# One-by-one row loads on two engines instead of one, with shared DMA semaphores and fewer gather buffers

## The chip, the cores and the metric

The kernel runs on one core of one Trainium2 chip. Times are device microseconds of that core. Five engines work beside each other, each through its own in-order queue: TensorE (PE; its weight loads are listed as PEld), VectorE (DVE), ScalarE (ACT), GpSimd (POOL) and the sync engine (SP). SP computes nothing; it issues DMAs. ScalarE can issue DMAs too, and GpSimd issues the indirect ones, whose source rows are given by a list of indices.

## The reference

One layer of a graph network: 12500 nodes with 128 features, 200000 edges sorted by their target node.

```python
h = jnp.maximum(_layernorm(x, axis=-1), 0.0)
msgs = h[src]
agg = jax.ops.segment_sum(msgs, dst, num_segments=n)
deg = jax.ops.segment_sum(jnp.ones((src.shape[0],)), dst, num_segments=n)
agg = agg / jnp.maximum(deg, 1.0)[:, None]
y = jax.nn.relu(agg @ Wg + h @ Ws + bg)
y = jnp.tanh(y @ W1 + b1)          # 128 -> 512
y = jnp.tanh(y @ W2 + b2)          # 512 -> 512
out = x + (y @ W3 + b3)            # 512 -> 128
```

All is float32. The irregular part is `h[src]`: 200000 rows of 512 bytes in the order of the edges.

## The kernel before

**Setup** (to about 111 us). The normalised rows h are computed in pieces and written to a table in DRAM, `htab`. The edge list is turned into columns, so that a column of `scol` holds the 128 source nodes of one chunk.

**Chunks.** The edges are cut into 1563 chunks of 128. Since the targets are sorted, a chunk's targets fall in a window of 144 nodes. For each chunk TensorE multiplies the 128 gathered rows by a 128 x 144 matrix of zeros and ones, which VectorE makes for groups of eight chunks (`onehot`, lines 360 to 383), and adds the product into a PSUM accumulator (`add`, line 422). 512 nodes are a block; 64 chunks feed one block. When its sums are complete, the block goes through the three layers (`part0` to `part4`, lines 516 to 583): matmuls on TensorE, with relu, tanh and bias on ScalarE between them.

**Where a chunk's rows come from.** There are three kinds.
- 1465 chunks are gathered: one indirect DMA of 128 rows each, issued by POOL (`gather`, line 301) into one of `AHEAD` = 48 buffers. A gather is issued up to 48 gathered chunks ahead of the add, and needs the buffer of an earlier chunk to be free.
- 80 raw chunks take rows of x itself, gathered at the start and normalised later.
- 18 "slow" chunks, one after every 72 gathered ones from chunk 160 on, are loaded row by row (`row_loads`, line 327). SP reads 32 row addresses into registers at a time (line 333), then, for each row, sets a register and issues a DMA of 512 bytes (line 341). Four buffers are kept for such chunks.

**The order of the work.** One loop over the chunks (line 632) writes the whole order out. In each turn it may issue a store, make the zeros and ones of a later group, issue gathers, let SP do its next four rows (line 655: one batch of four per 2.25 gathered chunks), add the chunk, and on every second chunk do one step of a block's layers. `keep_in_program_order` holds the instructions of TensorE, ScalarE and SP in this order, each on its own engine. SP's queue thus holds, mixed with the rows, the loads of `hb` and `xb` (h and x of a block) and the stores of `o` (results). From chunk `QUICK` = 1376 on, the layers' steps are placed by a small planner, which takes a chunk's rows to be there at 7.5 us plus 1.251 us for each gather before it (line 658), and a slow chunk's rows to be there already.

DMAs of SP and ScalarE count their completion on eight semaphores, taken in turn. A DMA waits until the last DMA on its semaphore, eight places earlier, has landed.

Of the kernel before, what the change touches and what calls it, by code (L numbers as in the profile page):

```python
# [22 lines left out]
F32 = mybir.dt.float32  # L23
# [8 lines left out]
P = 128  # L32
# [5 lines left out]
NRAW = 10  # L38
RAW0 = 256
STEP = 40  # L40
AHEAD = 48
SLOW0 = 160
EACH = 72
TOGETHER = 4
LOADS = 32
LATE = 12
LEAD = 16
QUICK = 1376
# [11 lines left out]
def windowed(ctx, tc, x, src, dst, Wg, Ws, bg, W1, b1, W2, b2, W3, b3, out, flag):  # L60
    nc = tc.nc
    N, D = x.shape
# [18 lines left out]
    def raw(c):  # L81
        return RAW0 <= c < RAW1 and (c - RAW0) % STEP < GRP


    slow, n = [], 0
    for c in range(SLOW0, NCH - 12):
        if raw(c):
            continue
        if n <= 0:
            slow.append(c)  # L90
            n = EACH
        else:
            n -= 1


    def first(w, span=per):
# [8 lines left out]
    blocks, n = [], 0  # L105
# [10 lines left out]
    rows_one = ctx.enter_context(tc.tile_pool(name="rows_one", bufs=4))  # L116
    rows_in = ctx.enter_context(tc.tile_pool(name="rows_in", bufs=AHEAD))
    ps_c = ctx.enter_context(tc.tile_pool(name="ps_c", bufs=1, space=PSUM))
# [8 lines left out]
    for t, a in ((rsrc, src), (rdst, dst)):  # L127
        a = a[RAW0 * P : RAW1 * P].rearrange("(u e) -> u e", u=NRAW)[:, : GRP * P]
# [46 lines left out]
    def centre(pool, xt, k, stats, bufs=2):  # L175
        nc.vector.tensor_reduce(stats[:, 0], xt, AX.X, ALU.add)
        nc.vector.scalar_tensor_tensor(xt, spread(stats[:, 0], k), -1.0 / D, xt, op0=ALU.mult, op1=ALU.add)
        sq = pool.tile([P, k, D], F32, name=f"sq{k}", bufs=bufs)
        nc.scalar.activation(sq, xt, AF.Square)
        nc.vector.tensor_reduce(stats[:, 1], sq, AX.X, ALU.add)  # L180

    def factors(stats):
        nc.scalar.activation(stats[:, 1], stats[:, 1], AF.Sqrt, bias=eps, scale=1.0 / D)
        nc.vector.reciprocal(stats[:, 1], stats[:, 1])
# [4 lines left out]
    with tc.tile_pool(name="setup", bufs=1) as sp, tc.tile_pool(name="ln", bufs=2) as ln:  # L189
# [59 lines left out]
        for c0, w in WINDOWS[1:]:  # L249
            v = low[:, c0:]  # L250
# [44 lines left out]
    def flat(t):  # L295
        return t.rearrange("p a b -> p (a b)")

    def sp_dma(*a):
        tc.keep_in_program_order(nc.sync.dma_start(*a))

    def gather(c):
        r = rows_in.tile([P, D], F32, name="rows")
# [7 lines left out]
    ROWB = 4 * D  # L310
    hbytes = htab.rearrange("n d -> (n d)").bitcast(U8)
# [3 lines left out]
    place = const.tile([len(slow), P], I32, name="place")  # L315
# [8 lines left out]
        def copy(*a):  # L324
            tc.keep_in_program_order(nc.scalar.copy(*a))

    def row_loads():
        for i, c in enumerate(slow):
            r = rows_one.tile([P, D], F32, name="srows")
            rows_t[c] = r  # L330
            rb = r.bitcast(U8)
            for p0 in range(0, P, LOADS):
                loads, vs = nc.values_load_multi_w_load_instructions(
                    place[i : i + 1, p0 : p0 + LOADS], engines=[mybir.EngineType.SP], min_val=0,
                    max_val=(N - 1) * ROWB,
                    skip_runtime_bounds_check_because="src holds rows of x, as the indirect DMAs take it to",
                )
                for ld in loads:
                    tc.keep_in_program_order(ld)
                for p, v in enumerate(vs, p0):  # L340
                    sp_dma(rb[p : p + 1, :], hbytes[bass.ds(v, ROWB)].rearrange("(o b) -> o b", o=1))
                    if (p + 1) % TOGETHER == 0:
                        yield

    def raw_stats(i):
        return stats_raw[:, :, i * GRP : (i + 1) * GRP]

    def raw_scaled(i):
        h = raw_rows[i]
        scale(h, h, GRP, raw_stats(i))  # L350
        for j in range(GRP):
            rows_t[RAW0 + i * STEP + j] = h[:, j]
# [11 lines left out]
    def onehot(g):  # L364
        k = min(GRP, NCH - g * GRP)
        lo, w = window(g * GRP)
        is_raw = raw(g * GRP)
        oh = ed.tile([P, GRP, W_RAW], F32, name="ohr", bufs=2) if is_raw else oh_bufs[g % OHS]
        if not is_raw and w < oh_w[g % OHS]:
            nc.vector.memset(oh[:, :, w : oh_w[g % OHS]], 0.0)  # L370
            oh_w[g % OHS] = w
        nc.vector.tensor_tensor(  # L372
            oh[:, :k, :w], lane[:, None, :w].to_broadcast([P, k, w]),
            dloc[:, g * GRP : g * GRP + k][:, :, None].to_broadcast([P, k, w]), op=ALU.is_equal,
        )
        ohs[g] = oh
        step, n = (oh.shape[2], w) if is_raw else (PITCH - per, w + per * (k - 1))
        cnt = ed.tile([P, PITCH], BF16, name="cnt", bufs=16)
        part, row, col = oh.ap
        shifted = bass.AP(tensor=oh.tensor, offset=oh.offset, ap=[part, [col[0], n], [step * col[0], k]])  # L380
        with nc.allow_low_precision(reason="whole numbers up to the chunks of a group"):
            nc.vector.tensor_reduce(cnt[:, :n], shifted, AX.X, ALU.add)  # L382
        counts[g] = (lo, n, cnt)
# [10 lines left out]
    def count(b):  # L394

        n, m = blocks[b]
        dg = flat(ps_m.tile([P, 4, P], F32, name="pm"))
        groups = sorted({c // GRP for c in reach[b]})
        for g in groups:
            lo, w, cnt = counts[g]  # L400
            a0, a1 = max(lo, n), min(lo + w, n + m)
            pe.matmul(
                dg[:, a0 - n : a1 - n], ones, cnt[:, a0 - lo : a1 - lo], start=(g == groups[0]), stop=(g == groups[-1]),
                skip_group_check=True,
            )
        rd = ml.tile([P, BLK], F32, name="rd", bufs=3)
        nc.vector.tensor_scalar(rd[:, :m], dg[:, :m], 1.0, None, op0=ALU.max)  # L407
        nc.vector.tensor_reduce(total[:, b : b + 1], dg[:1, :m], AX.X, ALU.add)
        nc.vector.reciprocal(rd[:, :m], rd[:, :m])  # L409
        rds[b] = rd  # L410
# [189 lines left out]
        )  # L600

    order = [c for c in range(NCH) if not raw(c) and c not in slow]
    loading = row_loads()
    work, done, nxt, behind = [], 0, 0, 0
    ngrp = -(-NCH // GRP)
    span = BLK // per
# [2 lines left out]
    def store(upto):  # L609
        while stores and stores[0][0] <= upto:  # L610
            sp_dma(*stores.pop(0)[1:])

    def soonest():
        two = work[: 2 if len(work) > 1 and work[1][3] < work[0][3] and work[0][4] else 1]
        return min(two, key=lambda w: max(w[2], now), default=None)
# [16 lines left out]
    for c in range(NCH):  # L632
        g = c // GRP
        at = c
        store(c if c >= QUICK else c - LATE)
        if c % GRP == 0 and g + 2 < ngrp:
            onehot(g + 2)
            if raw((g + 2) * GRP):
                raw_scaled(((g + 2) * GRP - RAW0) // STEP)
            if 2 <= g < 2 + NRAW:  # L640
                centre(ed, raw_rows[g - 2], GRP, raw_stats(g - 2), bufs=1)
            if g == 2 + NRAW:
                factors(stats_raw)

        while c % GRP == GRP // 2 and counted < len(blocks) and reach[counted][-1] // GRP <= g + (c >= QUICK):
            count(counted)
            counted += 1
        while nxt < len(order) and nxt < behind + AHEAD:
            gather(order[nxt])
            nxt += 1  # L650
        if not raw(c) and c not in slow:
            behind += 1
            batch = behind * P // (EACH * TOGETHER)
            if behind > SLOW0 - 3 * EACH and batch > (behind - 1) * P // (EACH * TOGETHER):
                next(loading, 0)
        if c >= QUICK:

            there = 7.5 + 1.251 * (NRAW * GRP + order.index(c)) if c not in slow else 0
            while soonest() and max(now, soonest()[2]) < there:
                go_on(soonest())  # L660
            now = max(now, there) + 0.27
        add(c)

        lead = LEAD if c < QUICK else 2
        if done < len(blocks) and (c - lead if across[done] else c) >= reach[done][-1]:
            if across[done]:
                merge(done)
            quick = reach[done][-1] + LEAD >= QUICK

            before = done - 1 if done and reach[done - 1][-1] + LEAD < QUICK else None  # L670
            work.append([layers(done, before), 0, 0, 0, quick and blocks[done][1] <= P])
            done += 1

        if c % span == span - 10 and (c // span + 1) * BLK < N:
            own_turned(c // span + 1)
            if (c // span + 2) * BLK < N:
                own(c // span + 2)
        if c < QUICK:
            if c % 2 == 0:
                go_on(work[0] if work else None)  # L680
        if c == QUICK:
            for b, (_, n) in enumerate(blocks):
                if n < BLK:
                    own_part(b)
# [379 lines left out]
```

## Time and profile before

| | |
|---|---|
| median of 15 runs | 2343.8 us (2334.72 to 2350.2) |
| the profiled execution | 2338.67 us, span 2336.7 us |
| mean TensorE clock granted | 0.784 of full speed |
| POOL: gathers from `htab` | 1465, first at 111.0, last at 2277.7 us |
| SP: row DMAs | 2304, first at 118.8, last at 2083.8 us |
| ScalarE: work | 226.8 us in 362 instructions |
| DMA engines, busy | 20% of the time between 111 and 2279 us |

How to read the lines of the profile: "busy" is an engine's own work; what a sequencer does (waits, register moves, issuing DMAs) is not counted there and stands under the queue's name with a q, as SPq. In a line of waits, the first name waited for the second: total us, times, longest. In a line of the order of time come start, duration, engine, source line, operation, result and operands, number of instructions, and in brackets the idle time before it and what ended that. In the view of one tile or source line the three durations are the shortest, the median and the longest in ns, then the first and last start in us. All matmuls and DMAs recorded by a helper carry that helper's line: L290 for matmuls, L299 for SP's DMAs, L322 for activations, L303 for gathers.

### The profile page before, as it was taken

Reading aid. Unit: us, or ns where it says so; the run is one execution under the profiler, and the core shown is the slowest. Engines: PE = TensorE matmul, PEld = TensorE weight load, DVE = VectorE, ACT = ScalarE, POOL = GpSimd, SP = SyncE. Lnnn points to the kernel's source line nnn. Section 1 sums busy time; section 2 is a strip of 40 time slices with the busy share of each in tenths; the row PEclk is TensorE's granted clock in tenths of the full one; section 3 lists DMA queues with packets and bytes.
Section 4 is the critical chain, followed back from the end, with each engine's and each line's share of the span. In section 5 each row is a group of like instructions: output and inputs, shape, how many; then the busy total and the mean of one; then the engine's idle time right before and its main releaser. Section 6 shows DMA issues by size and latency. Waiting matters only on the chain.

```text
span 2336.7 us, 19720 instructions
## 1 busy us (share of the span) xinstructions
PE 1330.9 (57%) x5212; PEld 872.7 (37%) x5212; DVE 1066.2 (46%) x651; ACT 226.8 (10%) x362; POOL 1463.9 (63%) x1553
## 2 busy tenths in 40 slices
PE   0132345567657766765565654555665566564768
PEld 0021233344335444443343333333333343332437
DVE  5924283455446545643353443434444444423432
ACT  1100010001111011100001000000000000010013
POOL 7675656666666666666666666666666666646660
PEclk9998577778878787787777777877777777776789
DMA  6721111212221222212222122222121221221210
GB/s 167 214 53 38 50 46 50 55 51 60 56 57 53 54 55 59 60 52 55 54 55 54 52 55 55 55 56 52 53 62 50 57 57 51 54 59 44 63 49 10
DMA packets 124131, 139.34 MB, mean 60 GB/s; under 512 B 32776, under 2 KB 98454, under 8 KB 123816
## 3 DMA queue, kind: packets, MB, share of 16 engines
q0 software_dynamic: 49440, 101.35, 16.6%
q1 hardware_dynamic: 71374, 33.32, 5.2%
q10 hardware_dynamic: 3196, 3.32, 0.6%
q8 instruction: 43, 0.70, 0.1%
q14 instruction: 78, 0.64, 0.1%
HBM read 125.06 MB, written 12.82 MB: 59 GB/s over the span
## 4 chain that ended last, share of the span: by engine, by line
PE 36%; another core or an unknown queue 25%; DVE 16%; issue 16%; POOL 5%; ACT 1%; DMA 0%; DVEq 0%; POOLq 0%; ACTq 0%
PE pm L290 22%; PE agg L290 9%; DVE cnt L382 7%; PE edge L290 5%; DVE oh L372 5%; POOL raw L146 3%; POOL rows L303 2%; DVE rd L409 2%; PE pt L293 1%; ACT h L322 1%; DVE o L579 0%; DMA rows<-htab,scol 0%; DVE mT L523 0%; DVE rd L407 0%
## 5 line engine op out<-in xcount | busy, mean ns | idle before, releaser
L303 POOL DMA_INDIRECT rows<-htab,scol x1465 | 1385.4, 946 | 788.5 <-issue 336.2
L290 PE MATMUL pm<-h,w 128*128 128x512 f32 (+4 forms) x1344 | 716.5, 628 | 172.5 <-ACT h L322 97.5
L372 DVE TENSOR_TENSOR oh<-shared,dloc 128x1152 f32<-128x1152 f32 (+2 forms) x186 | 243.5, 1315 | 875.0 <-remote 373.0
L290 PE MATMUL agg<-oh,rows 128*128 128x144 f32 (+3 forms) x2098 | 442.2, 330 | 261.3 <-issue 206.1
L290 PEld LDWEIGHTS agg<-oh,rows 128*128 128x128 f32 x2098 | 389.5, 226 | 511.3 <-issue 445.0
L382 DVE TENSOR_REDUCE cnt<-oh 128x200 bf16<-128x1600 f32 (+2 forms) x186 | 524.7, 2825 | 4.8
L290 PEld LDWEIGHTS pm<-h,w 128*128 128x128 f32 x1344 | 241.4, 218 | 214.6 <-issue 106.6
L290 PEld LDWEIGHTS edge<-oh,rows 128*128 128x128 f32 x832 | 152.4, 219 | 135.9 <-issue 131.3
L290 PE MATMUL edge<-oh,rows 128*128 128x144 f32 (+2 forms) x832 | 163.3, 317 | 28.9 <-issue 26.7
L293 PE MATMUL pt<-ident,hb 128*128 128x128 f32 x98 | 26.7, 411 | 265.5 <-DVE o L579 178.5
L322 ACT ACTIVATE h<-pm,b2c 128x512 f32<-128x512 f32 (+4 forms) x112 | 70.8, 633 | 694.5 <-PE agg L290 222.3
L293 PEld LDWEIGHTS pt<-ident,hb 128*128 128x128 f32 x98 | 16.7, 206 | 273.7 <-DVE o L579 182.9
L290 PE MATMUL pm<-mT,wg 128*128 128x512 f32 (+4 forms) x56 | 45.2, 904 | 104.0 <-DVE mT L523 82.5
L407 DVE TENSOR_SCALAR rd<-pm 128x512 f32<-128x512 f32 (+4 forms) x28 | 17.4, 621 | 175.6 <-remote 123.2
L322 ACT ACTIVATE h<-pm,b1c 128x512 f32<-128x512 f32 (+4 forms) x112 | 68.7, 632 | 259.8 <-remote 185.6
L146 POOL DMA_INDIRECT raw<-in_x_dram,rsrc x80 | 77.6, 970 | 25.6 <-issue 24.1
L409 DVE RECIPROCAL rd<-rd 128x512 f32<-128x512 f32 (+4 forms) x28 | 81.8, 2920 | 0.0
L290 PE MATMUL pm<-cnt,ones 128*128 128x200 bf16 (+7 forms) x294 | 30.5, 227 | 47.1 <-issue 46.9
L290 PEld LDWEIGHTS pm<-mT,wg 128*128 128x128 f32 x56 | 12.1, 268 | 110.2 <-DVE mT L523 86.3
L205 PE MATMUL pm<-ident,idx_f 98*128 98x98 f32 x32 | 6.2, 376 | 75.8 <-issue 75.8
L322 ACT ACTIVATE h<-pm,bgc 128x512 f32<-128x512 f32 (+4 forms) x28 | 17.7, 632 | 294.8 <-remote 120.3
L579 DVE TENSOR_TENSOR o<-pt,xb 128x512 f32<-128x512 f32 x23 | 15.8, 686 | 60.6 <-remote 45.0
(68 smaller groups left out, 509.9 us busy)
## 6 DMA issues: line engine op xcount, KB each, us to landing
srows<-htab SPq DMA_DIRECT2D x2304, 0.5 KB
rows<-htab,scol POOLq DMA_INDIRECT x1465
hb<-htab SPq DMA_DIRECT2D x24, 256.0 KB
xb<-in_x_dram SPq DMA_DIRECT2D x23, 256.0 KB
out_dram<-o SPq DMA_DIRECT2D x23, 256.0 KB
htab<-h SPq DMA_DIRECT2D x6, 896.0 KB
xt<-in_x_dram SPq DMA_DIRECT2D x5, 896.0 KB
raw<-in_x_dram,rsrc POOLq DMA_INDIRECT x80
```

Of the source, the lines that this page charges most:

```text
L146: nc.gpsimd.indirect_dma_start(out=t[:, j, :], out_offset=None, in_=x, in_offset=bass.IndirectOffsetOnAxis(ap=rsrc[:, g, j : j + 1], axis=0),)
L205: nc.tensor.transpose(p[:, q, :NROW], rf[:, (q0 + q) * P : (q0 + q + 1) * P], ident[:NROW, :NROW])
L290: tc.keep_in_program_order(nc.tensor.matmul(*a, **k))
L293: tc.keep_in_program_order(nc.tensor.transpose(*a, **k))
L303: nc.gpsimd.indirect_dma_start(out=r, out_offset=None, in_=htab, in_offset=bass.IndirectOffsetOnAxis(ap=scol[:, c : c + 1], axis=0),)
L322: tc.keep_in_program_order(nc.scalar.activation(*a, **k))
L372: nc.vector.tensor_tensor(oh[:, :k, :w], lane[:, None, :w].to_broadcast([P, k, w]), dloc[:, g * GRP : g * GRP + k][:, :, None].to_broadcas ...
L382: nc.vector.tensor_reduce(cnt[:, :n], shifted, AX.X, ALU.add)
L407: nc.vector.tensor_scalar(rd[:, :m], dg[:, :m], 1.0, None, op0=ALU.max)
L409: nc.vector.reciprocal(rd[:, :m], rd[:, :m])
L579: nc.vector.tensor_tensor(o[:, :whole], po[:, :whole], xb[:, :whole], op=ALU.add)
```

## The change

Row-by-row loading is done by two engines. From chunk 160 on, a chunk goes to SP after every 48 others (instead of 72), and to ScalarE after every 60 others, the first after 24, up to chunk 1436. That makes 27 chunks for SP (3456 rows) and 19 for ScalarE (2432 rows), and leaves 1437 for POOL. ScalarE's batches of four rows stand in its queue between the activations. Each engine has four buffers for such chunks; gather buffers go from 48 to 44. A new helper, `in_turn`, keeps all of these DMAs, of both engines, in one order for the assignment of semaphores: it adds an ordering mark without a wait between each such DMA and the one before it in the program. The index rows that ScalarE loads during setup (`at_i`, line 314) go from 18 to 46.

```diff
-AHEAD = 48
+AHEAD = 44
 SLOW0 = 160
-EACH = 72
+EACH = 48
+EACH_A = 60
...
-    slow, n = [], 0
+    slow_s, slow_a = [], []
+    ns, na = 0, EACH // 2
     for c in range(SLOW0, NCH - 12):
         if raw(c):
             continue
-        if n <= 0:
-            slow.append(c)
-            n = EACH
+        if ns <= 0:
+            slow_s.append(c)
+            ns = EACH
+        elif na <= 0 and c < QUICK + EACH_A:
+            slow_a.append(c)
+            na = EACH_A
         else:
-            n -= 1
+            ns -= 1
+            na -= 1
+    slow = slow_s + slow_a
...
+    turn = []
+
+    def in_turn(start):
+
+        tc.keep_in_program_order(start)
+        if turn:
+            tc.add_manual_dep(
+                start.ins, turn.pop(),
+                mybir.DependencyInfo(mybir.DependencyClass.NoSync, mybir.DependencyReason.DATA), reason="in_turn",
+            )
+        turn.append(start.ins.name)
+
     def sp_dma(*a):
-        tc.keep_in_program_order(nc.sync.dma_start(*a))
+        in_turn(nc.sync.dma_start(*a))
...
+        def dma(*a):
+            in_turn(nc.scalar.dma_start(*a))
+
-    def row_loads():
-        for i, c in enumerate(slow):
-            r = rows_one.tile([P, D], F32, name="srows")
+    def row_loads(chunks, engine, dma, name, together):
+        for c in chunks:
+            i = slow.index(c)
+            r = rows_one.tile([P, D], F32, name=name)
...
-                    if (p + 1) % TOGETHER == 0:
+                    dma(rb[p : p + 1, :], hbytes[bass.ds(v, ROWB)].rearrange("(o b) -> o b", o=1))
+                    if (p + 1) % together == 0:
                         yield
...
-    loading = row_loads()
+    loading = row_loads(slow_s, mybir.EngineType.SP, sp_dma, "srows", TOGETHER)
+    loading_a = row_loads(slow_a, mybir.EngineType.Activation, act.dma, "arows", TOGETHER)
...
             if behind > SLOW0 - 3 * EACH and batch > (behind - 1) * P // (EACH * TOGETHER):
                 next(loading, 0)
+            batch = behind * P // (EACH_A * TOGETHER)
+            if behind > 48 and batch > (behind - 1) * P // (EACH_A * TOGETHER):
+                next(loading_a, 0)
```

More of the change, by code (lines that the diff above doesn't have):

```diff
@@ L333, in row_loads @@
                 loads, vs = nc.values_load_multi_w_load_instructions(
-                    place[i : i + 1, p0 : p0 + LOADS], engines=[mybir.EngineType.SP], min_val=0,
-                    max_val=(N - 1) * ROWB,
+                    place[i : i + 1, p0 : p0 + LOADS], engines=[engine], min_val=0, max_val=(N - 1) * ROWB,
                     skip_runtime_bounds_check_because="src holds rows of x, as the indirect DMAs take it to",
@@ L340, in row_loads @@
                 for p, v in enumerate(vs, p0):
-                    sp_dma(rb[p : p + 1, :], hbytes[bass.ds(v, ROWB)].rearrange("(o b) -> o b", o=1))
-                    if (p + 1) % TOGETHER == 0:
+                    dma(rb[p : p + 1, :], hbytes[bass.ds(v, ROWB)].rearrange("(o b) -> o b", o=1))
+                    if (p + 1) % together == 0:
                         yield
```

## The prediction

> **What bounds the kernel now.** I read the page first, then the views of the sync engine's (SP's) queue, because the change is nearly all instructions that the page counts as no busy time.
>
> ```profile
> PE 1330.9 (57%) x5212; PEld 872.7 (37%) x5212; DVE 1066.2 (46%) x651; ACT 226.8 (10%) x362; POOL 1463.9 (63%) x1553
> ...
> L303 POOL DMA_INDIRECT rows<-htab,scol x1465 | 1385.4, 946 | 788.5 <-issue 336.2
> ```
>
> No engine is full. The gathers follow each other at best every 1.25 us (0.946 busy and 0.30 before the next), so 1465 of them need 1831 us of the 2168 us in which they run: POOL streams 85% of the time and pauses 337 us. The waits say who waits for whom:
>
> ```profile
> PEld agg L290 <- DMA rows<-htab,scol: 27.3, 37, 1.8
> ...
> PE pm L290 <- DMA srows<-htab: 0.3, 1, 0.3
> ```
>
> ```profile
> POOL rows L303 <- remote: 197.4, 137, 5.4
> POOL rows L303 <- PE agg L290: 136.5, 136, 17.5
> ```
>
> TensorE hardly ever waits for gathered rows (27 us); POOL waits for TensorE to free row buffers. So gathers are not simply late. The order of time shows what happens instead. POOL gathers without pause up to 1165 us, then stands still for 3.09 us:
>
> ```profile
> 1164.11 0.95 POOL L303 DMA_INDIRECT rows<-htab,scol  x1 [0.30 <-issue]
> 1168.14 0.95 POOL L303 DMA_INDIRECT rows<-htab,scol  x1 [3.09 <-remote]
> ```
>
> SP, in the same time, before and after 1167 us:
>
> ```profile
> 1153.63 5.00 SPq L299 DMA_DIRECT2D srows<-htab  x6
> 1158.65 0.71 SPq L299 DMA_DIRECT2D hb<-htab  x1
> 1160.76 7.03 SPq L299 DMA_DIRECT2D srows<-htab  x5
> ```
>
> ```profile
> 1167.10 4.12 SPq L299 DMA_DIRECT2D srows<-htab  x12
> ```
>
> While POOL streams, 11 rows take 13.5 us (1.22 us each); after the pause 12 rows take 4.12 us (0.34 each). In the stretch from 118 to 206 us, where POOL never pauses, SP's register moves last 700 ns in the median (first fence); over the whole run 29 ns (second):
>
> ```profile
> L299 SPq MOVE srows<-htab x32: 5/700/1398, 117.4 to 203.5; - x32
> ```
>
> ```profile
> L299 SPq MOVE srows<-htab x2304: 2/29/1426, 117.4 to 2083.7; - x192
> L299 SPq DMA_DIRECT2D srows<-htab x2304: 1/227/1400, 118.8 to 2083.8; - x192
> ```
>
> ```profile
> L333 SPq TENSOR_LOAD <-place x72: 294/2030/2555, 116.0 to 2067.6; - x72
> ```
>
> The main reading: SP issues rows from 118.8 to 2083.8 us, 2304 in 1965 us, 0.853 each with the value loads (2.03 us for 32 rows) and 66 larger DMAs. Does it wait in that time? By its own waits, very little:
>
> ```profile
> SPq L299 <- DMA srows<-htab: 46.1, 97, 1.4
> SPq L299 <- DVE o L579: 34.9, 6, 10.7
> ```
>
> About 80 us. SP is full, by issuing. Its last row belongs to the program's place c = 1394 (one batch of four per 2.25 gathered chunks), and TensorE adds chunk 1394 at about 2087 us: SP goes in step with TensorE, with nothing in hand.
>
> **The change, part by part.** Counted with the kernel's own rules, the slow chunks go from 18 to 27 (SP) and 19 (ScalarE), the gathers from 1465 to 1437.
>
> Removed, 28 gathers. At the pitch 35 us; with POOL's pauses (2168/1465 = 1.48) 41 us. That is worth something only if POOL still sets the pace.
>
> Added on SP, 9 chunks: 1152 register moves, 1152 DMAs and 36 value loads. One slow chunk costs SP (1965 - 45)/18 = 106.7 us at today's pace, 45 us being the other DMAs at about 0.7. The cheapest 128 rows of the run begin at 291.1 us and take 82.1 us, while POOL pauses more than usual. The program now asks for 3456 rows between places 16 and 1436, 1420 places. Today a place takes 1965/1392 = 1.41 us, so SP has 2003 us for them: 0.56 us a row after the 45, and no 128 rows of the trace went below 0.64. SP, full now, must fall behind, and TensorE then waits at its slow chunks. That wait has a return: with TensorE stopped, POOL fills its 44 buffers and pauses, and SP speeds up. I bound SP from both sides:
>
> - best pace seen: 27 x 82.1 + 45 = 2262 us;
> - today's pace, no relief: 27 x 106.7 + 45 = 2926 us;
> - mixed: in the 15.5% of pauses (305 of 1965 us) I take half at 0.34, since the first 2 us of a pause are still slow in the lines above. That is 447 rows; the other 1857 in 1813 us come to 0.98 each, loads and other DMAs included. One place needs 2.43 rows and brings 0.92 gathers, 1.15 us of streaming, which carries 1.17 rows; the missing 1.26 go at 0.40 (0.34 and a share of the load) in pauses, 0.50 us. A place costs 1.65 us, SP 1420 x 1.65 = 2343 us.
>
> I take 2300, between the best pace and the mixed sum, because both describe a POOL that is stopped often.
>
> Added on ScalarE, 19 chunks between places 48 and 1307: 2432 moves and DMAs and 76 value loads, in batches of four between the activations. A batch holds the activations behind it by 1.4 us (0.34 a row) to 4.9 us (1.22). It has 1.93 rows a place, and its activations and copies (about 8.6 us per 64 places) 0.14 us. By the same sum 1.01 us of streaming carry 1.03 rows and the other 0.90 go at 0.40: 1.51 us a place, under SP's 1.65. So SP sets the pace, and the held activations lie inside SP's wait. If that cover goes, it costs up to 608 batches x 3.4 us less ScalarE's idle time: rival 2.
>
> The transfers of the added rows, 0.5 KB each, cost 0: the DMA engines are busy a fifth of the time.
>
> Semaphores shared in program order: an SP row now waits for the DMA eight places earlier, which may be ScalarE's, and the other way round. Behind the waiting row on SP stand hb, xb and the stores of o; behind it on ScalarE the tanh that TensorE needs next. So SP can't lag behind ScalarE up to place 1307; from there to 1436 TensorE may run ahead, 129 x 0.2 = 26 us back. Price of the waits themselves: 0 (46 us in 97 waits today, beside issue) up to rival 2.
>
> Setup: 28 more index rows on ScalarE. Between 28 x 0.26 = 7 us and 28 x 2.0 = 57 (the 18 of today stretch from 33.1 to 69.6 us); most lies beside VectorE, busy 69% there. I take 10. The 44 buffers for 48: 0, inside the wait for SP, at most 337 x 48/44 - 337 = 31 if POOL were the bound. TensorE and VectorE do the same work on either kind of chunk: 0 both ways, as the shapes are the same. The late chunks' due times in the planner fall by up to 28 x 1.25 = 35 us, which reorders work in the last 253 us: taken as 0, between -20 and +20.
>
> Sum: SP reaches place 16 at about 150 us (TensorE adds chunk 25 at 161 us), plus 10; 2300 for the rows; minus 26; then what today follows place 1436, 253 - 42 x 1.41 = 194 us. Together 2628 against a span of 2336.7. The profiled execution took 2338.7, 0.2% under the median of 2343.8, so I say **2630 us**, 12% slower. No change would be 0.2% either way, about what a measurement here can tell.
>
> A rule of the Trainium skill speaks for the change: Perfetto Trace Analysis, Identifying the Most-Contended Engine, says to relieve the engine with the highest occupancy first. That is POOL at 63%, and by it the time would be about 2300. The trace disagrees, since SP's full queue has no occupancy at all. The same page, DMA Instruction — HWDGE, says that two issuing sequencers share one descriptor generator under a lock. An estimate by it and the 227 ns row is 5888 x 0.227 = 1337 us, no bound by itself; no run here yet shows two queues of rows at once.
>
> **Rivals.**
> 1. Lag is allowed. Rows are issued some 92 places before their use, so TensorE may run ahead of SP by about 60 places, until hb is missing. With the best pace: 160 + 2262 - 85 + 194 = 2530, and down to 2400 if long pauses bring a row to 0.60. For it: POOL and TensorE wait for nothing else. Against: the shared semaphores tie SP to ScalarE.
> 2. The two queues hold each other up: a batch of ScalarE waits for SP, TensorE for the tanh behind it. At today's pace without relief: 160 + 2926 - 80 + 194 = 3200; halfway to my sum, 2900. For it: activations already wait 644 us for events the trace can't name. Against: the return through POOL's pauses.
> 3. Faster: SP keeps up after all. Place: the rows between two pauses. It decides from 0.56 us a row on, with POOL still at 85%. Price: 28 x 1.48 = 41 us gained, 2300. For it: 0.34 after a pause, 52 rows at 0.46 from 313 us. Against: no 128 rows below 0.64.
> 4. The change doesn't do what it says: the order ties the queues so closely that rows go one at a time. At the 0.46 of the best stretch, 5888 x 0.46 + 354 = 3060.
>
> **How the numbers follow.** My case 0.60 (2450 to 2850), rival 1 0.14 (2390 to 2530), rival 2 0.12, rival 4 0.04, rival 3 (faster) 0.09, no change 0.01. The range from 2390 to 2980 leaves out rivals 3 and 4, no change, and half of rival 2: 0.20. Slower: 0.90.
>
> **What will show it.** Right: SP rows from 140 to about 2440 us at 0.6 to 0.7 each, TensorE and ScalarE waiting on srows or on row semaphores, POOL's pauses twice as long or more, its pitch in streams still 1.25. Wrong: SP's rows ending near 2100 with POOL still streaming 85%; or ScalarE full and SP waiting for it, which is rival 2.

## The result, and the profile after

The changed kernel takes 2703.9 us (median of 10 runs, 2692.3 to 2714.4) against 2343.3 us before: a ratio of 1.153, 95% interval 1.152 to 1.155. The forecast was 2630 us with a range from 2390 to 2980, slower with a chance of 0.90. The direction and the bound were right; the time was 2.7% too low.

The profiled execution took 2701.9 us, with a span of 2699.8 us. From the page, the busy time of each engine, and from the groups, the gathers and the matmuls of the layers (busy us and mean ns, then idle time before them and what ended it):

```profile
PE 1332.3 (49%) x5212; PEld 890.4 (33%) x5212; DVE 1068.3 (40%) x651; ACT 228.0 (8%) x362; POOL 1436.9 (53%) x1525
...
L322 POOL DMA_INDIRECT rows<-htab,scol x1437 | 1358.8, 946 | 1181.8 <-PE agg L297 529.8 <-issue 323.8 <-remote 182.5
L297 PE MATMUL pm<-h,w 128*128 128x512 f32 (+4 forms) x1344 | 740.7, 651 | 721.6 <-ACT h L341 470.9 <-issue 162.1 <-DVE total L430 68.3
```

The computing engines do the work of before, to within about 2%, and POOL does less; all their shares fall. The gathers run from 117.0 to 2643.7 us. At 1.25 us each they need 1796 us, 71% of that stretch, and POOL pauses 731 us where it paused 337 before. The first cause of those pauses has become TensorE (529.8 us; 136.5 before).

The rows, from the views of the tiles `srows` (SP) and `arows` (ScalarE): shortest, median and longest in ns, then first and last start in us.

```profile
L318 SPq MOVE srows<-htab x3456: 2/29/1406, 119.4 to 2575.7; - x192
L318 SPq DMA_DIRECT2D srows<-htab x3456: 2/228/1447, 119.5 to 2575.7; - x192
```

```profile
L347 ACTq DMA_DIRECT2D arows<-htab x2432: 3/228/1410, 290.6 to 2335.9; - x188
```

SP issues rows from 119.5 to 2575.7 us: 2456 us for 3456 rows, 0.711 us each. Only 47 us of that stretch lie in gaps of more than 1.5 us in front of an instruction. SP is full, as it was before, and now until 124 us before the end (253 us before). Full does not mean busy with rows alone. In the same stretch 977 gaps of 0.4 to 0.8 us, 654 us together, lie between its instructions. They stand in front of register moves, which wait for no semaphore, nearly as often (447) as in front of row DMAs (505), so most are not waits for rows to land. The waits on record say the same of SP, and show who else waits for rows:

```profile
SPq L318 <- DVE o L601: 77.6, 3, 59.0
SPq L318 <- DMA srows<-htab: 71.5, 149, 1.5
SPq L318 <- DMA arows<-htab: 50.5, 25, 32.4
```

```profile
ACT h L341 <- DMA arows<-htab: 773.6, 100, 43.2
POOL rows L322 <- PE agg L297: 529.8, 168, 49.0
PE pm L297 <- ACT h L341: 496.9, 60, 58.7
...
ACT h L341 <- DMA srows<-htab: 478.0, 35, 28.7
```

The third line of the second fence was 97.5 us in 23 waits before. How one of these waits comes about is seen in the order of time. ScalarE, SP, TensorE and POOL at the same moment:

```profile
1218.64 0.69 ACT L341 ACTIVATE h<-pm,b2c 128x512 f32<-128x512 f32 x1 [19.45 <-issue]
1222.92 18.93 ACTq L347 DMA_DIRECT2D arows<-htab  x20
1241.90 0.69 ACT L341 ACTIVATE h<-pm,bgc 128x512 f32<-128x512 f32 x1 [22.57 <-DMA arows<-htab]
```

```profile
1214.85 18.53 SPq L318 DMA_DIRECT2D srows<-htab  x22
1233.43 0.40 SPq L318 DMA_DIRECT2D xb<-in_x_dram  x1
1233.93 32.91 SPq L318 DMA_DIRECT2D srows<-htab  x60
```

```profile
1242.64 2.07 PE L297 MATMUL pm<-h,w 128*128 128x512 f32 x2 [20.23 <-ACT h L341]
```

```profile
1225.40 0.95 POOL L322 DMA_INDIRECT rows<-htab,scol  x1 [0.30 <-issue]
1245.47 0.95 POOL L322 DMA_INDIRECT rows<-htab,scol  x1 [19.13 <-PE agg L297]
```

SP spends 18.5 us on 22 rows, 0.84 us each. ScalarE needs the same time for 20 rows of its own, which stand in one order of semaphores with SP's, and the relu behind them starts at 1241.9 us. TensorE has stood for 20.2 us waiting for it, and POOL for 19.1 us waiting for TensorE. Once POOL has stood for a while SP gets faster: 60 rows in 32.9 us, 0.55 each. In all, ScalarE spends 635 us in gaps of over 1.5 us in front of its own row DMAs (168 times); the 1410 us left of its stretch are 0.58 us a row, activations included.

### The profile page after: what moved, and what is told of

It reads as the page before. It is cut to its first block, busy times and chain, and to the rows that moved or that the text cites. A ratio compares the mean times of both kernels' runs of the same rounds, so it can differ in the third digit from the quotient of the medians.

```text
span 2699.8 us, 27041 instructions
## 1 busy us (share of the span) xinstructions
PE 1332.3 (49%) x5212; PEld 890.4 (33%) x5212; DVE 1068.3 (40%) x651; ACT 228.0 (8%) x362; POOL 1436.9 (53%) x1525
## 5 line engine op out<-in xcount | busy, mean ns | idle before, releaser
L322 POOL DMA_INDIRECT rows<-htab,scol x1437 | 1358.8, 946 | 1181.8 <-PE agg L297 529.8
L297 PE MATMUL pm<-h,w 128*128 128x512 f32 (+4 forms) x1344 | 740.7, 651 | 721.6 <-ACT h L341 470.9
L297 PEld LDWEIGHTS agg<-oh,rows 128*128 128x128 f32 x2070 | 405.9, 241 | 357.0 <-issue 308.7
L297 PEld LDWEIGHTS edge<-oh,rows 128*128 128x128 f32 x804 | 141.7, 212 | 132.0 <-issue 122.6
L297 PE MATMUL edge<-oh,rows 128*128 128x144 f32 (+2 forms) x804 | 151.8, 308 | 33.7 <-issue 30.9
L297 PE MATMUL agg<-sums,ident 128*128 128x140 f32 (+4 forms) x108 | 27.5, 396 | 140.8 <-ACT sums L344 87.8
L300 PE MATMUL pt<-ident,hb 128*128 128x128 f32 x98 | 19.6, 332 | 112.7 <-DVE o L601 42.9
L297 PEld LDWEIGHTS agg<-sums,ident 128*128 128x128 f32 x108 | 21.2, 267 | 144.8 <-ACT sums L344 89.8
L297 PE MATMUL pm<-mT,wg 128*128 128x512 f32 (+4 forms) x56 | 35.9, 729 | 57.9 <-DVE mT L545 31.3
L297 PEld LDWEIGHTS <-ones 128*128 128x128 bf16 x294 | 27.5, 116 | 109.2 <-issue 108.1
```

Of the source, the lines that this page charges most:

```text
L297: tc.keep_in_program_order(nc.tensor.matmul(*a, **k))
L300: tc.keep_in_program_order(nc.tensor.transpose(*a, **k))
L322: nc.gpsimd.indirect_dma_start(out=r, out_offset=None, in_=htab, in_offset=bass.IndirectOffsetOnAxis(ap=scol[:, c : c + 1], axis=0),)
```

## The experiments

Each ratio is against the kernel before on the same chip. That kernel took 2326 us on two of the chips, 2345 us on a third and 1953.8 us on the chip of the last run, of which more below. Kernels from different chips are compared by their ratios; the kernel after, at 1.153, would be 2683 us where before takes 2326. Before these runs two theories stood against each other: A, SP's issuing of rows sets the pace and all other waits are its consequences; B, the activations held behind ScalarE's own rows set it.

### SP's 27 chunks alone

```diff
-        elif na <= 0 and c < QUICK + EACH_A:
+        elif False:
```

> The changed kernel with ScalarE's 19 chunks given back to POOL's gathers; SP keeps its 27. Theory A (SP's issuing of 3456 rows sets the pace): 2530 to 2680 us, SP's rows at 0.65 to 0.72 us each, close to the changed kernel's 2704. Theory B (activations held behind ScalarE's rows set it): 2300 to 2400 us.

Measured: 2646.7 us, ratio 1.139 (1.137 to 1.142). SP's part alone makes 13.9 of the 15.3% that the whole change costs, 320 of 357 us at this chip's 2326.5. Theory A holds. SP issues its rows from 110.3 to 2501.7 us, 0.692 us each, with no gap of over 1.5 us:

```profile
L318 SPq DMA_DIRECT2D srows<-htab x3456: 1/228/1397, 110.3 to 2501.7; - x192
```

But TensorE does not wait for an activation behind rows any more. It waits for `hb`, the block's h, whose load stands behind rows in SP's queue:

```profile
ACT hT L344 <- PE pt L300: 552.4, 19, 56.8
PE pt L300 <- DMA hb<-htab: 530.9, 17, 41.7
```

In the kernel after, that wait is 37 us:

```profile
PE pt L300 <- DMA hb<-htab: 37.2, 1, 37.2
```

So some 500 us of waiting change their place and nearly all of the loss stays: what stops TensorE is wherever SP's lateness reaches it first.

### ScalarE's 19 chunks beside SP's old load

```diff
-EACH = 48
+EACH = 72
...
-    ns, na = 0, EACH // 2
+    ns, na = 0, 24
```

> The changed kernel with SP back at 18 chunks (every 72) and ScalarE at its 19. Theory A: SP asks for no more than before, ScalarE's 1.51 us a place is a little over today's 1.41, so 2350 to 2500 us. Theory B: 2600 us or more, nearly the changed kernel.

Measured: 2400.5 us, ratio 1.033 (1.029 to 1.037), inside A's bounds and far from B's. SP's 2304 rows take 0.896 us each, and SP now waits for ScalarE's rows:

```profile
SPq L318 <- DMA arows<-htab: 136.3, 31, 43.3
```

### ScalarE's chunks alone

```diff
-        if ns <= 0:
+        if False:
```

> ScalarE's 19 chunks alone, none on SP (the 27 are gathered). Theory A, an engine whose queue has time left pays little: ScalarE has 2432 rows of some 0.7 us, 1700 us, and some 300 us of other work, which goes into 2100 us; 2330 to 2400 us, less than the 2400 of the kernel with 18 chunks on SP beside them. Theory B, activations held behind batches of rows cost TensorE more than the gathers save: 2420 us or more.

Without SP's list the count gives ScalarE 20 chunks, 2560 rows. Measured: 2357.2 us, ratio 1.014 (1.009 to 1.019), as theory A has it. Against 18 chunks on SP the 20 on ScalarE cost 31 us more; against no row loads at all (below, 1.004) about 1%. The rows take 0.705 us each. Activations do wait for them (the line below), and for all that the time is only 1% longer: TensorE waits 99.6 us for ScalarE's `h` here, 97.5 us before and 496.9 us after.

```profile
ACT h L341 <- DMA arows<-htab: 448.5, 76, 17.7
```

### No row loads at all

```diff
-        if n <= 0:
+        if False:
...
```

(in the kernel before; the index rows for them are left out too, and all 1483 chunks are gathered)

> The kernel before without row loads at all: its 18 chunks are gathered by POOL too (1483 gathers). If a gather is worth its pitch with pauses (1.48 us): 2343 + 27 = 2370 us. If SP's row instructions slow the other engines: below 2343. If POOL's gathers are hidden behind other work: 2343 within 5.

Measured: 2338.9 us (10 runs), ratio 1.0044 (1.0019 to 1.0069). That is 4 to 16 us more than before on this chip, between the first expectation and the last. The 18 slow chunks of the kernel before gain some 10 us, 0.6 us each, not the 1.48 us of a gather's share of the time. POOL streams 86% of the time here and pauses 306 us. At that price the change could have hoped for 28 x 0.6 = 16 us.

### 22 chunks on SP instead of 18

```diff
-EACH = 72
+EACH = 60
```

(in the kernel before)

> The kernel before with a slow chunk after every 60 others: 22 chunks on SP instead of 18, nothing on ScalarE. Theory A, SP has nothing in hand: by a straight line between 18 chunks (2327 us on that chip) and 27 (2647), 35.6 us for each chunk more, 2470 us; at least 2400. Rival, SP's pace gives way first, because long pauses of POOL bring a row to 0.69 us: 2816 rows x 0.69 + 255 = 2200 us would fit into the time of before, and the time stays within 2320 to 2345 us.

Measured: 2425.3 us, ratio 1.044 (1.039 to 1.050). Four chunks more cost 99 us, 25 us each, and the next five 221 us, 44 each: less than the straight line at first, but theory A's 2400 us are passed and the rival's room is not there. From the slow chunks' times in the traces it can be seen what is used up first. The table gives the time from the issue of a slow chunk's last row on SP to TensorE's add of that chunk.

| kernel | first six chunks | later | last |
|---|---|---|---|
| before (18) | 124 to 145 us | 99 to 142 | 126 |
| 22 on SP | 109 to 138 | 45 to 101 | 86 |
| 27 on SP | 78 to 126 | 28 to 91 | 74 |
| after (27 and 19) | 137 to 160 | 123 to 170, the 26th 98 | 82 |

With SP alone the lead shrinks: TensorE runs ahead of SP until `hb` is missing. This happens once, and is worth as much as the tail after SP's last row gets shorter: from 253 us to 142 (22) and 139 (27). The span's growth against before splits accordingly (the trace of before is from a chip on which that kernel takes 17 us more). 22 chunks: rows 210 us longer, tail 111 shorter, first row 12 earlier, +87. 27 chunks: rows 426 us longer, tail 114 shorter, first row 9 earlier, +304. The first 110 us of lateness were free, and with 22 chunks they are used up.

A chunk more thus takes 52 us of SP's time (22 chunks) or 47 (27), some 0.4 us a row, less than half of the mean of before, 0.853. From 18 to 27 chunks, the gathers that POOL begins while SP loads rows go from 1323 to 1398, 94 us more of streaming; the other 332 us are pauses of POOL. So most of the time that SP needs more is time in which POOL stands.

### SP's rows from fixed addresses

```diff
-                loads, vs = nc.values_load_multi_w_load_instructions(
+                if engine == mybir.EngineType.SP:
+                    loads, vs = [], [(c * P + p) % N * ROWB for p in range(p0, p0 + LOADS)]
+                else:
+                    loads, vs = nc.values_load_multi_w_load_instructions(
...
-                    dma(rb[p : p + 1, :], hbytes[bass.ds(v, ROWB)].rearrange("(o b) -> o b", o=1))
+                    dma(rb[p : p + 1, :], (hbytes[v : v + ROWB] if isinstance(v, int) else hbytes[bass.ds(v, ROWB)]).rearrange("(o b) -> o b", o=1))
```

> The changed kernel, but SP's rows come from fixed addresses: no value loads and no register move before each DMA; the same number of DMAs, semaphores and bytes. It leaves out the right rows for SP's 27 chunks. Theory A (the number of SP instructions is what costs): SP's row falls from 0.71 to 0.35 to 0.45 us, and the time to 2400 to 2550, where ScalarE sets it. Theory B, or DMAs alone costing: 2650 to 2710.

Measured: 2377.7 us, ratio 1.022 (1.019 to 1.026). The same 3456 DMAs of SP, with no register moves and no value loads, bring the loss from 15.3% down to 2.2%. SP has time left now: 325 us in gaps of over 1.5 us between its first row and its last, where the kernel after has 47. Its longest wait is for ScalarE's rows:

```profile
SPq L318 <- DMA arows<-htab: 138.4, 73, 53.4
```

```profile
L318 SPq DMA_DIRECT2D srows<-htab x3456: 2/223/1465, 116.7 to 2205.1; - x192
```

Both figures of theory A were missed all the same: a row takes 0.604 us with those gaps and 0.51 without them, not 0.35 to 0.45, and the time is under 2400 us. The number of DMAs and their bytes are those of the kernel after; only SP's instructions became fewer (and its rows come from other places of the table). That is the strongest of the runs for theory A: the price is in SP's instructions. How it divides between register moves and value loads no run shows.

### Without the shared order of the semaphores

```diff
-        if turn:
-            tc.add_manual_dep(
-                start.ins, turn.pop(),
-                mybir.DependencyInfo(mybir.DependencyClass.NoSync, mybir.DependencyReason.DATA), reason="in_turn",
-            )
-        turn.append(start.ins.name)
```

> The kernel after, without the ordering marks between the DMAs of SP and ScalarE. Theory A1, the shared semaphores are what 19 chunks on ScalarE add on top of SP's 27 chunks (2704 against 2647 us): the time falls to 2630 to 2665 us. Theory A2, the 57 us come from the activations held by ScalarE's own issuing, and the order of the semaphores is worth nothing: 2690 to 2715 us.

Measured: 2753.1 us, ratio 1.182 (1.178 to 1.187). The 57 us that both theories set out from were the difference of two chips; by the ratios ScalarE's chunks add 1.4% to SP's, 33 us. And neither theory holds: without the marks the kernel is 2.5% slower than the kernel after (1.182 against 1.153). SP's rows take 0.730 us each. Activations wait behind ScalarE's rows and, as with SP alone, TensorE waits for `hb`:

```profile
ACT h L335 <- DMA arows<-htab: 520.9, 83, 19.2
PE pt L300 <- DMA hb<-htab: 464.5, 19, 36.8
```

So the program's order of the semaphores is no price but a help of 2.5%. The run does not untie the queues: all eight semaphores serve both here too (each 425 to 437 of SP's rows and 299 to 309 of ScalarE's), only in another order. What the sharing itself costs no run shows. What it is that makes SP's row cheaper with the marks, 0.711 against 0.730, is not settled.

### Fewer gather buffers

```diff
-AHEAD = 48
+AHEAD = 44
```

(in the kernel before; likewise 32 and 24, and 24 in the kernel after)

> The kernel before with 44 gather buffers in place of 48, nothing else. The prediction took 0 for this, at most 31 us: 2327 us on the chip of the other runs, up to 2358 if POOL's buffers set the pace of before. A rival: fewer buffers give SP shorter streams of POOL and so more time, then 2310 to 2325.

Measured: 2320.2 us (10 runs), ratio 0.9973 (0.9955 to 0.9990), in the rival's range.

> The kernel before with 32 gather buffers: between 44 (2320 us) and 24 under either theory; 2300 to 2318 us by theory A, 2330 to 2350 by the rival.

Measured: 2333.0 us, ratio 0.9945 (0.9926 to 0.9965).

> The kernel before with 24 gather buffers in place of 48. 44 gave 0.27% less than 48. Theory A, shorter streams of POOL let TensorE, SP and ScalarE go faster: 2285 to 2315 us. Rival, buffers are what holds POOL up in before: 2340 us or more.

Measured: 2330.8 us, ratio 0.9939 (0.9918 to 0.9960). The expectations for 32 and 24 buffers were set by a chip on which before takes 2327 us; by the ratios the two are 2314 and 2313 us there, inside theory A's ranges, though the second only by 2 us.

> The kernel after with 24 gather buffers in place of 44. Theory A, SP's rows set the pace and are slow while POOL streams: with 24 buffers POOL fills its buffers sooner after each stop of TensorE and pauses earlier and in shorter pieces, so SP gets a faster pace at the same rows; 0.64 to 0.69 us a row, 2540 to 2680 us. Rival, the length of the streams is nothing to SP, and fewer buffers leave TensorE without rows after each stop: 2710 to 2900 us.

Measured: 2696.4 us, ratio 1.152 (1.148 to 1.155), not to be told from the kernel after, and outside both expectations; SP's row takes 0.704 us. So the number of buffers is not what holds POOL up, and a quicker stop of POOL does not make SP's rows cheaper by more than 1%. The kernel before with 24 or 32 buffers is 0.6% faster than before and the fastest found here. Why is open: SP's row takes 0.842 us with 24 and 0.854 with 32, where before takes 0.853.

### An eighth of the gathers

```diff
-            gather(order[nxt])
+            if nxt % 8 == 0:
+                gather(order[nxt])
+            else:
+                rows_t[order[nxt]] = rows_t[order[nxt - 1]]
```

(in the kernel after)

> The kernel after, with seven gathers of eight left out (180 instead of 1437; the other chunks are added with the rows of the gather before, so the sums are not the reference's). Rows of SP and ScalarE, matmuls and activations are all as after. Theory A, a row costs SP 0.71 us because POOL streams beside it (fast rows take 0.32 us, and 128 of them with their loads at best 0.52): with POOL streaming a tenth of the time rows fall to 0.35 to 0.50 us, SP's 3456 rows need 1200 to 1750 us and don't set the end any more; 1600 to 2200 us in all. Rival, two queues of rows beside each other cost 0.6 to 0.7 us a row by themselves: SP still needs 2100 us or more, and the time is 2350 us or more.

Measured: 1844.7 us. SP's rows take 0.473 us each. Both numbers are theory A's, and yet the run doesn't show what it was made for, because it fell on a chip where the kernel before, with all its gathers, takes 1953.8 us (7 runs, 1952.8 to 1954.9) at a clock of 0.907, where the other chips grant 0.78 to 0.79. Whether it was the gathers left out or the chip that made the rows cheap can't be told. The view of `srows` shows that no register move is slow here, where the longest took 1.4 us in the other runs:

```profile
L318 SPq MOVE srows<-htab x3456: 29/29/29, 98.9 to 1734.9; - x192
L318 SPq DMA_DIRECT2D srows<-htab x3456: 224/228/366, 98.9 to 1735.0; - x192
```

Some of it speaks for the chip. Taking only the stretches in which POOL has streamed for more than 6 us, in which 40% (before) and 32% (after) of SP's and ScalarE's moves for rows last over 300 ns, this run has 93 moves, and none is slow.

One thing the run does show. Even at 0.473 us a row SP stands in gaps of over 1.5 us for only 73 of 1636 us, and the span ends 102 us after its last row: 3456 rows with their moves fill SP's queue though POOL streams for only 225 us. The part of the expectation that says that SP wouldn't set the end any more was wrong.

## Why the prediction was right

**The bound.** "SP is full, by issuing" was the reading on which all stood, and the runs bear it out: rows on SP alone cost 13.9 of the 15.3%, and with fewer instructions for the same DMAs on SP 2.2% are left. No page of busy times shows it. The rule weighed in the prediction, to relieve the engine with the highest occupancy (the Trainium skill, Perfetto Trace Analysis, Identifying the Most-Contended Engine), would have had 2300 us; POOL was relieved of 28 gathers, its share fell from 63% to 53%, mostly because the time rose by 15%.

**The sum, term by term.** SP's first row: 150 + 10 us predicted, 119.5 measured. It belongs to the program's place 16, but SP does not issue it in step with TensorE's adds: it goes out as early as the first row of before (118.8). Rows: 2300 predicted, 2456 measured. Tail after SP's last row: 194 - 26 = 168 predicted, 124 measured; the lead of the table falls from about 152 us to 82, so 70 are given back where 26 were taken, some of them before ScalarE's list ends. In all -40 + 156 - 44 = +72 us, the 2699.8 of the trace against 2628.

The mis-sized term is the rows. SP's stretch begins 40 us earlier and ends 44 us nearer the end than predicted. So 84 of its 156 us are the other two errors counted with the opposite sign, and their cancelling is no luck. POOL begins 1387 gathers in that stretch. The line of `--windows` has busy us and number of instructions of PE, PEld, DVE, ACT and POOL in this order, then the granted clock:

```profile
119.50:2575.70 2456.20, 1235.91 (x4654) 814.81 (x4653) 947.39 (x523) 184.67 (x278) 1311.51 (x1387) 0.75 0.17 46
```

The prediction's 1420 places bring 1420 x 0.92 = 1306. Its mixed sum, 1.65 us a place, 2343 us in all, was made of 1633 us of streaming and 710 of pauses. Measured were 2456 / 1420 = 1.73 us a place: 1387 x 1.25 = 1734 us of streaming and 722 of pauses. So the mixed sum is short by 113 us, 101 of them for 81 gathers that SP's longer stretch takes in. That its pauses come out so close is in part luck: SP issued 2128 rows while POOL streamed, 0.82 us each where 0.98 was taken, and 1327 in the pauses, 0.54 each where 0.40 was taken.

The step that failed is "I take 2300, between the best pace and the mixed sum". It makes 43 of the 72 us; with 2343 the forecast would have been 2671, 1.1% under the trace. The best 128 rows of a run are no end toward which the average goes: the kernel after has a best stretch too, 0.522 us a row, and an average of 0.711.

**ScalarE under SP.** "So SP sets the pace, and the held activations lie inside SP's wait" holds to 1.4%: with SP's chunks alone the ratio is 1.139, with both 1.153. With SP's queue in time, ScalarE's chunks do have a price of their own (1% alone, 3.3% beside SP's 18), smaller than rival 2 feared and not the 0 that was taken.

**Semaphores.** "Price of the waits themselves: 0" is neither shown nor refuted, since no run takes the sharing away. The order of the semaphores costs nothing: without it the kernel is 2.5% slower. That SP "can't lag behind ScalarE" fits the table of leads, 130 us and more until ScalarE's last row at 2336 us; without the marks they fall to about 50.

**The rivals.** Rival 1, lag allowed, is a fair picture of SP's chunks alone: TensorE runs ahead until `hb` is missing, and wins about 114 us in the tail (85 predicted); only the row pace was again too good, so that it ends at 2647 and not at 2530 us. The reading that SP had "nothing in hand" left out this lead. In the kernel after it is kept nearly until ScalarE's list ends. Rival 2's chain (ScalarE behind SP, TensorE behind the tanh) is there to be seen in the fences, at a price of 1.4% and not of the hundreds of us that rival 2 added. That the return through POOL's pauses bounds it is the prediction's argument, which no run tests by itself. Rival 3 was decided at 0.56 us a row; 0.711 were reached. Rival 4, the order of the queues as the brake, fell with the run without the marks, which is slower, and with SP's chunks alone, which need nearly the same time with no second queue. The mean of both queues together, 2456 / 5888 = 0.42 us a row, would not have told it from the 0.46 that rival 4 took.

**Small terms.** Removed gathers: 28 x 1.48 = 41 us were said to be worth something only if POOL set the pace; by the run without row loads a gather is worth 0.6 us even in the kernel before. Buffers: 0 taken, at most 31; 44 buffers in the kernel before gave -6 us. Setup: 10 us taken, the first gather comes 6 us later and SP's first row 0.7 us later. POOL's pauses "twice as long or more": 2.2 times, with its pitch in streams still 1.25. The row signs missed by a little: SP's rows ran from 119.5 to 2575.7 us at 0.711, not from 140 to about 2440 at 0.6 to 0.7.

**One generator for two queues.** The Trainium skill's page Perfetto Trace Analysis, DMA Instruction — HWDGE, says that the sequencers it covers share one descriptor generator under a lock. The estimate by it was 1337 us and no bound, and no run shows one: ScalarE's 2432 rows with SP's 3456 at fixed addresses cost 1.022.

## What to carry to other kernels

Look for a full queue among the sequencers, not only for a busy engine: count its instructions, moves and value loads included, divide the stretch by them, and see how little of it is waiting. Work that is taken from a streaming engine is worth what a run without the old piece of it shows (here 0.6 us per gather), not its share of the time; what it costs at a full queue is what that queue's time grows by for each piece more (here 47 to 52 us per chunk of 128 rows), which can be far from the queue's mean price (here 107 us per chunk before).
A lead of one engine over another hides lateness once, by its own length; past that each further row costs in full, and it shows at whatever the late queue holds next (here `hb`, or a tanh).
For the mean pace of a full queue take the mix over all its work, not a place between that and its best stretch.

## What was not expected of the hardware

- The chips differ. The same kernel before takes 2326 to 2345 us on three of them and 1953.8 us on a fourth. 1465 gathers at 1.25 us are 1831 us, which leaves 123 us there for the start and the end: POOL can hardly pause on that chip. If POOL's stream is the bound there, the change would take 28 x 1.25 = 35 us off, an estimate from those numbers; the kernel after was not run on that chip, so that the ratio of 1.153 is shown for the others only.
- While POOL streams, register moves of SP and ScalarE that take 29 ns otherwise often take 700 to 1400 ns, in every trace but that of the run with an eighth of the gathers, the only trace from the fourth chip. In the kernel after, 32% of the moves are slow once POOL has streamed for 6 us, and 4 of 1505 once it has paused for 2 us. POOL pauses mostly when TensorE stands, so the trace does not tell which of the two it is, and what in the chip does it was not found.
- These stalls hardly go by the number of rows. With 18, 22 and 27 chunks on SP alone (2304, 2816 and 3456 rows), SP's queue has 1047, 1098 and 1080 gaps of 0.4 to 0.8 us and 522, 560 and 556 moves of over 300 ns, while POOL streams for 1654, 1761 and 1748 us of SP's stretch (1.25 us for each gather begun in it). That fits the low price of a further row.
- Taking gather buffers away made the kernel before a little faster, 0.3% with 44 and 0.6% with 24.
